# Routing in four parts instead of three, experts an earlier unit, and four more units masked by GpSimd

## The chip, the cores and the metric

One core of a Trainium2 chip runs the whole layer. The metric is the device time of one execution in microseconds. Three runs of the kernel before gave 662.93, 663.86 and 665.39 us.

## The reference, cut to what matters

4096 tokens (16 sequences of 256) of 128 channels are normalised, and the result goes into two branches whose outputs are added to the input: causal attention with 16 heads of 8 channels and a second layernorm, and a mixture of 8 experts of which each token takes its best two.

```python
xn  = layernorm(x)                                     # x: 16 x 256 x 128
Q, K, V = relu(xn @ Wq + bq), relu(xn @ Wk + bk), relu(xn @ Wv + bv)
att = softmax(causal(Q_h @ K_h.T / sqrt(8))) @ V_h     # 16 heads, rows whose sum of xn is 0 masked
att = layernorm(att + xn) * gamma + beta
h   = rms_weight * xn * rsqrt(mean(xn*xn) + 1e-6)
top_w, top_i = top_k(softmax(h @ gate_w.T), 2)         # weights scaled to sum 1
moe = sum over the two experts e: top_w * (silu(h @ w1[e].T) * (h @ w3[e].T)) @ w2[e].T
out = x + att + xn + moe
```

## The kernel before, in words

Tokens are cut into 32 tiles of 128, four tiles are a block (two sequences), so there are 8 blocks. Attention runs over 16 units: unit `u` is block `u // 2` with one half of the heads. A unit has these steps in a hand-written order: `weights(u, 0..2)` (scores transposed, with the maximum already folded in, and their exponentials `e` by ScalarE, L858), `scores(u+1, 0..2)` (scores of the next unit, only to find the row maxima: `tops`, L774 and L782 on VectorE), `values(u, 0..1)` (exponentials times V, `O`, copied to `oT` by ScalarE, L897), `finish(u, 0..1)` (division, second layernorm's statistics) and `queries(u+1)` (the maxima added to the queries, `Qs`, L800). The order of TensorE's instructions is the order of the program; a scheduler orders the other engines, with some orders fixed by hand (`behind`, `issue_after`).

In between, `fill()` is called seven times a unit and doles out other work by small budgets:

- `early_work` runs `prepared()`: for each chunk of tiles in `CHUNKS` the layernorm `normed` (ends with a square root by three Newton steps in `newton_sqrt`), and when the logits of a part in `ROUTES` are there, `route` (best two experts of each token, positions in the experts' lists by two small matmuls `pos_ps` and `taken_ps`, L548 to L555) and `planned` (which tiles of 256 list rows a wave of experts has). Each `yield` names its cost, and a fill may spend `EARLY_US` of it; `PAUSE` ends the fill's share. `logit_step` turns a normed block (`lT`, L662) and multiplies it with the gate (L657) one fill later.
- `masks` runs `exact`, an exact remainder of the layernorm that block n's attention needs; before the attention of a new block starts, what it needs is forced (in the even units).
- `spaced_rows` scatters tokens' rows into the experts' lists in DRAM by GpSimd (`lists<-rows`, L608, two per tile), `ROWS_BESIDE` of them per fill, held behind the last exponential.
- `experts` takes one step per `1 / EXPERT_STEPS` fills. An expert tile `i` (36 tiles of 256 rows are always worked) takes three steps: `deliver` of tile i-2 (`R_ps`, `fres`, two scatters with addition into `places`, L1137), the first half of `up` (`AG`, L1100), `down` of tile i-1 (`Y`, L1117), turning of tile i+1 (`hT_ps`, L1089), the second half of `up`. `fetch(i)` loads the rows of tile i from the lists (`frows`, SyncE's queue, L1068) and the three weights; if the plan of tile i is not there yet, it forces `early_work`, and it forces all scatters of the parts that the tile's wave needs. `WAVES` follows from `ROUTES`: tile i belongs to the first wave whose routed tokens must fill it.
- `rest` does the second layernorm's last part (L1195 to L1202).

The experts' generator is made in unit `EXPERTS_FROM` and starts `EXPERTS_BEHIND` steps in debt. After the last unit the experts that are left run alone, with two steps of `rest` after each of theirs; then `places` is read back (`z`, L1345), added (L1349) and written out. In units before `POOL_MASKS` the causal mask of the exponentials is added by TensorE before the exponential (L847, 12 small bf16 matmuls with the identity a unit); from there on GpSimd zeroes the masked exponentials afterwards (L861, 6 selects a unit), and `values` waits for them.

Of the kernel before, what the change touches and what calls it, by code (L numbers as in the profile page):

```python
# [26 lines left out]
def tile_attention_plus_moe(  # L27
# [47 lines left out]
    NR = H // (HG * NG)  # L75

    ONE, OFF = 16, 18
    CHUNKS = [(0, 4), (4, 16), (16, 32)]
    ROUTES = [(0, 16), (16, 24), (24, 32)]
    RT = 16  # L80

    FIRST_US, EARLY_US, MASK_US, EXPERT_STEPS = 4.5, 1.4, 1.0, 1.08
    EXPERTS_FROM, EXPERTS_BEHIND = 2, 3
    ROWS_BESIDE = [3, 2, 1]
    POOL_MASKS = 7
    QSCALE = float(DH) ** -0.5
    SL = 256
    NTILES = (2 * NTOK + E * (SL - 1)) // SL  # L90
# [193 lines left out]
    def newton_sqrt(yv, w, tag):  # L284

        s = small.tile([P, w], F32, tag=f"{tag}s", name=f"{tag}_s")
        V.tensor_scalar(s[:].bitcast(U32), yv.bitcast(U32), 1, None, ALU.logical_shift_right)
        V.tensor_scalar(s[:].bitcast(U32), s[:].bitcast(U32), float(0x1FBD1DF5), None, ALU.add)
        rr = small.tile([P, w], F32, tag=f"{tag}r", name=f"{tag}_r")
        for _ in range(3):  # L290
            yield 0.8
            V.reciprocal(rr, s)
            V.tensor_tensor(rr, rr, yv, ALU.mult)
            V.tensor_tensor(s, s, rr, ALU.add)
            V.tensor_scalar(s, s, 0.5, None, ALU.mult)
        V.reciprocal(rr, s)
        return s, rr

# [7 lines left out]
    def misc(name):  # L306
        return psM.tile([P, BW], F32, tag="misc", name=name)
# [45 lines left out]
    PAUSE = None  # L353
# [136 lines left out]
    def route(t0, t1):  # L490

        n, nt = f"c{t0}", t1 - t0
        rs = rstd[:, t0:t1]
        lg = small.tile([P, nt, E], F32, tag="rlg", name=f"rlg_{n}")
        V.tensor_tensor(
            lg, lraw[:, t0:t1, :], rs.unsqueeze(2).to_broadcast([P, nt, E]), ALU.mult
        )

        sel = norm.tile([P, 2, nt, E], F32, tag="rsel", name=f"rsel_{n}")
        mx = small.tile([P, 2, nt], F32, tag="rmx", name=f"rmx_{n}")  # L500
        nth = small.tile([P, nt, E], F32, tag="rnth", name=f"rnth_{n}")
        for r in range(2):
            V.tensor_reduce(mx[:, r, :], lg, AX.X, ALU.max)
            V.tensor_tensor(
                sel[:, r], lg, mx[:, r, :].unsqueeze(2).to_broadcast([P, nt, E]), ALU.is_equal
            )
            yield 0.6
            V.tensor_tensor_scan(
                nth.rearrange("p t e -> p (t e)"),
                of_token[:, 0:nt, :].rearrange("p t e -> p (t e)"),  # L510
                sel[:, r].rearrange("p t e -> p (t e)"),
                0.0,
                ALU.mult,
                ALU.add,
            )
            V.scalar_tensor_tensor(sel[:, r], nth, 1.0, sel[:, r], ALU.is_equal, ALU.mult)
            if r == 0:
                V.scalar_tensor_tensor(lg, sel[:, r], MASKED, lg, ALU.mult, ALU.add)
            yield 0.9

        wts = small.tile([P, 2, nt], F32, tag="rwts", name=f"rwts_{n}")
        ex = small.tile([P, nt], F32, tag="rex", name=f"rex_{n}")
        V.tensor_tensor(ex, mx[:, 1, :], mx[:, 0, :], ALU.subtract)
        S.activation(ex, ex, AF.Exp)
        yield 0.2

        mine_bf = small.tile([P, E, nt], BF16, tag="rmine", name=f"rmine_{n}")
        V.tensor_tensor(
            mine_bf,
            sel[:, 0].rearrange("p t e -> p e t"),  # L530
            sel[:, 1].rearrange("p t e -> p e t"),
            ALU.add,
        )
        upto = small.tile([P, E, nt], BF16, tag="rupto", name=f"rupto_{n}")
        V.tensor_tensor_scan(
            upto.rearrange("p e t -> p (e t)"),
            going[nt].rearrange("p e t -> p (e t)"),
            mine_bf.rearrange("p e t -> p (e t)"),
            0.0,
            ALU.mult,  # L540
            ALU.add,
        )
        V.tensor_scalar(wts[:, 0, :], ex, 2.0, 2.0, ALU.mult, ALU.add)
        V.reciprocal(wts[:, 0, :], wts[:, 0, :])
        V.tensor_tensor(wts[:, 1, :], wts[:, 0, :], ex, ALU.mult)
        yield PAUSE
        pp = misc(f"pos_ps_{n}")[:, : E * nt]
        T.matmul(  # L548
            pp, lhsT=behind_bf, rhs=mine_bf.rearrange("p e t -> p (e t)"), start=True, stop=False
        )  # L550
        T.matmul(
            pp, lhsT=ones_bf, rhs=upto.rearrange("p e t -> p (e t)"), start=False, stop=True
        )
        tp = misc(f"taken_ps_{n}")[:, :E]
        T.matmul(tp, lhsT=ones_bf, rhs=upto[:, :, nt - 1], start=True, stop=True)  # L555
        begin = small.tile([P, E], F32, tag="rbegin", name=f"rbegin_{n}")
        V.tensor_tensor(begin, taken, list_start, ALU.add)
        V.tensor_tensor(taken, taken, tp, ALU.add)
        pos = small.tile([P, nt, E], F32, tag="rpos", name=f"rpos_{n}")
        V.tensor_tensor(  # L560
            pos,
            pp.rearrange("p (e t) -> p t e", e=E),
            begin.unsqueeze(1).to_broadcast([P, nt, E]),
            ALU.add,
        )
        yield 0.6
        pick = norm.tile([P, 2, nt, E], F32, tag="rpick", name=f"rpick_{n}")
        at = small.tile([P, 2, nt], F32, tag="rat", name=f"rat_{n}")
        at_u = small.tile([P, 2, nt], U32, tag="ratu", name=f"ratu_{n}")
        V.tensor_tensor(pick, sel, pos.unsqueeze(1).to_broadcast([P, 2, nt, E]), ALU.mult)  # L570
        V.tensor_reduce(at, pick, AX.X, ALU.add)
        V.tensor_copy(at_u, at)
        yield 1.1
        part = ROUTES.index((t0, t1))
        rows_left.append((part, scattered(part, t0, at_u, wts)))
# [658 lines left out]
    def fill(k_next=0):  # L1234

        logit_step(normed_upto[1])
        normed_upto[1] = normed_upto[0]
        due["early"] += EARLY_US if tiles_at else FIRST_US
        while due["early"] > 0:
            cost = beside(early_work)  # L1240
            if not cost:
                due["early"] = 0.0
            else:
                due["early"] -= cost
        due["masks"] = min(due["masks"] + MASK_US, 2 * MASK_US)
        while due["masks"] > 0 and exact_upto[0] < rooted_upto[0]:
            due["masks"] -= beside(masks)
        spaced_rows()
        for _ in range(k_next):
            next(side["next"], None)  # L1250
        due["experts"] += EXPERT_STEPS
        while due["experts"] >= 1:
            due["experts"] -= 1
            next(side["experts"], None)
        beside(side["rest"])
# [18 lines left out]
    for u in range(len(units)):  # L1274
        n, r = units[u]
        more = u + 1 < len(units)

        due_next = [0, 0, 0, 0, 1, 1, 1] if r == 0 else [1, 1, 1, 1, 0, 0, 0]
        if u == EXPERTS_FROM:
            side["experts"] = experts(ffn_pool, 0, USUAL)  # L1280
            due["experts"] = -EXPERT_STEPS * EXPERTS_BEHIND
        weights(u, 0)
        for _ in first:
            pass
        fill(due_next[0])
        if more:
            scores(u + 1, 0)
        fill(due_next[1])
        if u == EXPERTS_FROM:
            next(side["experts"])  # L1290
        weights(u, 1)
        fill(due_next[2])
        if more:
            scores(u + 1, 1)
        fill(due_next[3])
        if more:
            scores(u + 1, 2)
        o0 = values(u, 0)
        if r == 0 and n + 1 < NB:
            while exact_upto[0] < n + 2:  # L1300
                logit_step()
                beside(masks if rooted_upto[0] > n + 1 else early_work)
            side["next"] = projected(n + 1)
        fill(due_next[4])
        weights(u, 2)
        finish(u, 0, o0)
        if more:
            queries(u + 1)
        fill(due_next[5])
        o1 = values(u, 1)  # L1310
        exps.pop((u, 0))
        fill(due_next[6])
        finish(u, 1, o1)
        if r == 0 and n in (5, 7):
            for _ in side["rest"]:
                pass
            side["rest"] = rest(0, 4) if n == 5 else rest(4, 6)
    side["rest"] = chain(side["rest"], rest(6, 8))
    for _ in side["experts"]:
        for _ in range(2):  # L1320
            next(side["rest"], None)
    for _ in side["rest"]:
        pass

# [78 lines left out]
```

## Time and profile before

| | us |
|---|---|
| median of three runs | 663.86 |
| profiled execution, whole | 665.17 |
| its span in the profile | 663.30 |
| TensorE busy (matmuls) | 545.0 |
| VectorE busy | 435.9 |
| ScalarE busy | 337.8 |
| GpSimd busy | 246.6 |

The profile starts 1.87 us short of the device time. The first exponential of each unit starts at 50.05, 101.47, 141.50, 178.19, 218.09, 263.24, 298.89 and 331.74 us (units 0 to 7); unit 15 starts at 600.04 us. "Before 50 us" is the first block's layernorm, "after 623.9 us" the last experts alone and the way out.

### The profile page before, as it was taken

The numbers are of one execution on the slowest core, as the hardware profiler recorded it, in microseconds if no ns is written. First come the engines' busy times: TensorE is split into PE (matmuls) and PEld (weight loads), VectorE is DVE, ScalarE is ACT, GpSimd is POOL, SyncE is SP. The second block draws the span as 40 slices with busy tenths as digits, with TensorE's granted clock in tenths as the row PEclk, the third lists the DMA queues.
The fourth block names the chain that finished last, engine by engine and source line by source line (L and its number), as shares of the span: only waits on it lengthen the run. The fifth ranks groups of instructions, "written<-read, shape, count | busy, mean of one in ns | idle before, by whom it ended". The sixth has DMA issues, their size and how long they took to land. (4 is left out here: it accounts for less than half of the span.)

```text
span 663.3 us, 9975 instructions
## 1 busy us (share of the span) xinstructions
PE 545.0 (82%) x3293; PEld 323.9 (49%) x3293; DVE 435.9 (66%) x1171; ACT 337.8 (51%) x677; POOL 246.6 (37%) x287
## 2 busy tenths in 40 slices
PE   0377867687998968999999999899989998999940
PEld 0134523234665545556555655565655565566620
DVE  6757686576378675667666766786587656575943
ACT  1524597145735615555556456545668554445620
POOL 4240027460012554445352434243524244435450
PEclk9997669777999979999999999999999999999975
DMA  7200001015122342354323323332333223234128
GB/s 200 94 1 0 1 13 45 28 41 162 51 50 55 82 95 66 86 127 129 67 65 69 102 59 62 70 100 59 63 70 96 50 71 75 65 93 116 17 21 257
DMA packets 45892, 49.33 MB, mean 74 GB/s; under 512 B 5840, under 2 KB 38224, under 8 KB 45840
## 3 DMA queue, kind: packets, MB, share of 16 engines
q1 hardware_dynamic: 30112, 37.40, 18.8%
q0 software_dynamic: 12416, 8.99, 9.8%
q10 hardware_dynamic: 3312, 2.30, 1.2%
q8 instruction: 27, 0.44, 0.3%
q14 instruction: 25, 0.20, 0.1%
HBM read 34.16 MB, written 14.50 MB: 73 GB/s over the span
## 5 line engine op out<-in xcount | busy, mean ns | idle before, releaser
L1137 POOL DMA_INDIRECT places<-fres,frows x72 | 115.1, 1599 | 172.1 <-DVE fres L1133 143.1
L1100 PE MATMUL AG<-hT,w 128*112 128x256 f32 x576 | 140.0, 386 | 6.0 <-PE R_ps L1131 3.8
L1100 PEld LDWEIGHTS AG<-hT,w 128*112 128x112 f32 x576 | 98.5, 178 | 38.8 <-issue 9.9
L858 ACT ACTIVATE e<-W 128x1024 f32<-128x1024 f32 x96 | 93.3, 1020 | 46.4 <-PE W L847 27.7
L782 DVE TENSOR_REDUCE tops<-S 128x4 f32<-128x1024 f32 x64 | 75.3, 1217 | 37.2 <-PE S L760 26.7
L1109 DVE SCALAR_TENSOR_TENSOR th<-th,AG 112x512 f32<-112x512 f32 x72 | 49.4, 686 | 71.5 <-ACT th L1108 68.0
L608 POOL DMA_INDIRECT lists<-rows,ratu_c x64 | 64.1, 1001 | 57.8 <-ACT e L858 28.3
L1117 PE MATMUL Y<-hid,w 112*128 112x256 f32 x288 | 72.9, 397 | 13.8 <-ACT oT L897 5.0
L861 POOL TENSOR_SCALAR_AFFINE_SELECT e<-e 128x512 f32<-128x512 f32 (+1 forms) x54 | 49.6, 977 | 86.0 <-ACT e L858 85.7
L1108 ACT ACTIVATE th<-AG 112x512 f32<-112x512 f32 x72 | 42.8, 594 | 61.9 <-PE AG L1100 57.8
L747 PE MATMUL S<-KTm,QT 32*128 32x256 f32 (+1 forms) x512 | 67.9, 543 | 6.7 <-DVE tops L782 4.9
L832 PE MATMUL W<-Qm,KT 32*128 32x512 f32 (+1 forms) x512 | 65.6, 550 | 9.1 <-DVE tops L774 4.9
L1117 PEld LDWEIGHTS Y<-hid,w 112*128 112x128 f32 x288 | 53.7, 195 | 29.5 <-ACT oT L897 6.6
L1111 DVE TENSOR_TENSOR hid<-th,AG 112x512 f32<-112x512 f32 x72 | 48.9, 679 | 1.6
L897 ACT COPY oT<-O 128x512 f32<-128x512 f32 x32 | 18.7, 584 | 60.3 <-PE O L887 41.9
L774 DVE TENSOR_REDUCE tops<-S 128x8 f32<-128x1024 f32 x32 | 37.7, 1218 | 12.8 <-remote 8.1
L747 PEld LDWEIGHTS S<-KTm,QT 32*128 32x128 f32 x512 | 29.7, 193 | 33.1 <-issue 12.8
L876 PE MATMUL O<-e,vstat 128*32 128x512 f32 x256 | 36.3, 639 | 5.1 <-ACT yT L1125 2.6
L760 PE MATMUL S<-cmask,ident_bf 128*128 128x256 bf16 (+1 forms) x192 | 38.7, 327 | 0.0
L832 PEld LDWEIGHTS W<-Qm,KT 32*128 32x128 f32 x512 | 25.9, 195 | 25.2 <-issue 6.7
L1125 ACT COPY yT<-Y 128x256 f32<-128x256 f32 x36 | 13.3, 370 | 45.8 <-PE Y L1117 43.4
L760 PEld LDWEIGHTS <-ident_bf 128*128 128x128 bf16 x192 | 15.3, 100 | 36.7 <-issue 32.4
(236 smaller groups left out, 768.6 us busy)
## 6 DMA issues: line engine op xcount, KB each, us to landing
w<-in_w1T_dram SPq DMA_DIRECT2D x36, 224.0 KB
w<-in_w3T_dram SPq DMA_DIRECT2D x36, 224.0 KB
w<-in_w2T_dram SPq DMA_DIRECT2D x36, 224.0 KB
frows<-lists SPq DMA_DIRECT2D x36, 130.0 KB
places<-nought SPq DMA_DIRECT2D x8, 256.0 KB
lists<-filling SPq DMA_DIRECT2D x9, 130.0 KB
places<-fres,frows POOLq DMA_INDIRECT x72
lists<-rows,ratu_c POOLq DMA_INDIRECT x64
```

What stands on the lines that cost most here:

```text
L608: ins = G.indirect_dma_start(out=lists, out_offset=bass.IndirectOffsetOnAxis(ap=at_u[:, r, b - t0 + t : b - t0 + t + 1], axis=0), in_=rows ...
L747: T.matmul(out, lhsT=QT[rows, q0 : q0 + P], rhs=KTm[rows, :, b * SEQ : b * SEQ + nk], start=(part < 2 or b == 0), stop=False, skip_group_c ...
L760: T.matmul(out, lhsT=ident_bf, rhs=cmask[:, 0, :].unsqueeze(1).to_broadcast([P, 4 if part == 2 else 2, P]), start=False, stop=True, skip_g ...
L782: ins = V.tensor_reduce(of_heads[:, :, part, 1, :], pairs[g // 2].rearrange("p g (j k) -> p g j k", j=HG), AX.X, ALU.max, negate=True,).ins
L832: T.matmul(out, lhsT=KT[rows, k0 : k0 + P], rhs=Qm[rows, :, k0 : (b + 1) * SEQ], start=(part > 0 or b == 0), stop=on_pool and (part > 0 or ...
L858: ins = S.activation(two, pairs[g // 2], AF.Exp).ins
L861: behind["POOL"] = G.affine_select(on, on, [[0, 2 * nd], [1, P]], ALU.is_ge, no_weight, base=0, channel_multiplier=-1).ins
L1100: T.matmul(to[:, ts(c, SL)], lhsT=wt[:, 0, ts(2 * k + c, CI)], rhs=hT, start=True, stop=True,)
L1109: V.scalar_tensor_tensor(th, th, 1.0, ap, ALU.add, ALU.mult)
L1111: V.tensor_tensor(h, th, gp, ALU.mult)
L1117: T.matmul(yp, lhsT=w2[:, 0, c, :], rhs=hid[c // 2][:, ts(c % 2, SL)], start=(c == 0), stop=(c == NCI - 1),)
L1137: ins = G.indirect_dma_start(out=places, out_offset=bass.IndirectOffsetOnAxis(ap=rows[:, a, C : C + 1].bitcast(U32), axis=0), in_=res[:, a ...
```

## The change

Four things are edited, and constants with them.

1. `CHUNKS` goes from three chunks of 4, 12 and 16 tiles to four of 4, 8, 8 and 12; `ROUTES` from parts of 16, 8 and 8 tiles to parts of 12, 8, 8 and 4. The waves of expert tiles become [5, 13, 21, 39] instead of [9, 17, 39]. `EARLY_US` goes from 1.4 to 2.2, and a part after the first pauses once more before its position matmuls.
2. The experts' generator is made after fill 5 of unit 1 and at once takes its first step (the fetch of tiles 0 and 1), two steps in debt; before, it was made in unit 2, fetched after its second fill, three steps in debt.
3. `POOL_MASKS` goes from 7 to 3: units 3 to 6 are masked by GpSimd too.
4. A Newton step of the square root has two fused VectorE instructions and a reciprocal instead of three instructions and a reciprocal. After the last unit one step of `rest` follows each expert step instead of two.

```diff
-    CHUNKS = [(0, 4), (4, 16), (16, 32)]
-    ROUTES = [(0, 16), (16, 24), (24, 32)]
-    RT = 16
+    CHUNKS = [(0, 4), (4, 12), (12, 20), (20, 32)]
+    ROUTES = [(0, 12), (12, 20), (20, 28), (28, 32)]
+    RT = 12
...
-    FIRST_US, EARLY_US, MASK_US, EXPERT_STEPS = 4.5, 1.4, 1.0, 1.08
-    EXPERTS_FROM, EXPERTS_BEHIND = 2, 3
-    ROWS_BESIDE = [3, 2, 1]
-    POOL_MASKS = 7
+    FIRST_US, EARLY_US, MASK_US, EXPERT_STEPS = 4.5, 2.2, 1.0, 1.08
+    EXPERTS_FROM, EXPERTS_BEHIND = 1, 2
+    ROWS_BESIDE = [3, 2, 2, 1]
+    POOL_MASKS = 3
...
         for _ in range(3):
-            yield 0.8
+
+            yield 0.6
             V.reciprocal(rr, s)
-            V.tensor_tensor(rr, rr, yv, ALU.mult)
-            V.tensor_tensor(s, s, rr, ALU.add)
-            V.tensor_scalar(s, s, 0.5, None, ALU.mult)
+            V.scalar_tensor_tensor(rr, yv, 0.5, rr, ALU.mult, ALU.mult)
+            V.scalar_tensor_tensor(s, s, 0.5, rr, ALU.mult, ALU.add)
...
         yield PAUSE
+        if t0 > 0:
+            yield PAUSE
         pp = misc(f"pos_ps_{n}")[:, : E * nt]
...
-        if u == EXPERTS_FROM:
-            side["experts"] = experts(ffn_pool, 0, USUAL)
-            due["experts"] = -EXPERT_STEPS * EXPERTS_BEHIND
         weights(u, 0)
...
-        if u == EXPERTS_FROM:
-            next(side["experts"])
         weights(u, 1)
...
         fill(due_next[5])
+        if u == EXPERTS_FROM:
+            side["experts"] = experts(ffn_pool, 0, USUAL)
+            next(side["experts"])
+            due["experts"] = -EXPERT_STEPS * EXPERTS_BEHIND
         o1 = values(u, 1)
...
     for _ in side["experts"]:
-        for _ in range(2):
-            next(side["rest"], None)
+        next(side["rest"], None)
```

Built, the two programs differ in their order as follows. In unit 0 TensorE has three turned blocks of logits instead of four ahead of `xnT_1`. The first expert matmul (`AG` of tile 0) stands in unit 2 after the first `scores` part instead of after the second; at the start of unit 7 the new order has one half of `up` and one `down` more behind it, at the start of unit 15 two halves of `up`. The logits of blocks 4 to 7 move from units 2 and 3 to units 1, 2 and 4. On ScalarE the eight L1195 of the last two blocks stand behind the last expert's tanh instead of ahead of it.

## The prediction

> **What bounds the kernel now.** I read the page's 40 slices first, to see where TensorE has no work.
>
> ```profile
> PE   0377867687998968999999999899989998999940
> DVE  6757686576378675667666766786587656575943
> POOL 4240027460012554445352434243524244435450
> PEclk9997669777999979999999999999999999999975
> ```
>
> From slice 16 (265 us) to slice 37 TensorE is busy nine tenths at full clock: there only fewer matmuls shorten the run. From 33 to 265 us no engine is full, and the clock granted to TensorE is often 0.6 or 0.7. The windows of the units say how far each is from full (columns: us, busy of PE, PEld, DVE, ACT, POOL, then clock, DMA share, GB/s).
>
> ```profile
> 50.00:101.50 51.50, 39.60 (x201) 20.76 (x198) 38.24 (x148) 34.37 (x93) 4.99 (x9) 0.70 0.02 6
> 101.50:141.50 40.00, 27.90 (x144) 12.67 (x143) 24.58 (x66) 15.80 (x33) 24.82 (x30) 0.80 0.12 39
> 141.50:178.20 36.70, 31.45 (x186) 16.79 (x185) 20.58 (x53) 22.56 (x50) 4.83 (x5) 0.89 0.34 104
> 178.20:218.10 39.90, 36.30 (x247) 23.12 (x246) 29.05 (x109) 19.23 (x37) 9.02 (x9) 1.00 0.22 48
> 218.10:263.20 45.10, 36.51 (x220) 22.36 (x219) 30.04 (x93) 20.39 (x41) 23.70 (x26) 0.92 0.34 85
> 263.20:298.90 35.70, 33.63 (x220) 20.76 (x219) 22.49 (x63) 20.71 (x43) 15.29 (x17) 1.00 0.44 103
> 298.90:331.70 32.80, 31.69 (x206) 19.48 (x204) 23.22 (x51) 17.31 (x31) 15.43 (x13) 1.00 0.39 97
> ```
>
> Units 0 to 4 are the expensive ones. Who waited for whom, with the longest single wait last:
>
> ```profile
> DVE tops L774 <- remote: 8.1, 1, 8.1
> ACT oT L897 <- remote: 15.8, 2, 8.0
> PE hT_ps L1089 <- DMA frows<-lists: 3.6, 1, 3.6
> PE Y L1117 <- DVE hid L1111: 4.7, 1, 4.7
> ```
>
> The first two are two holes, at 118 to 126 us (unit 1) and 235 to 243 us (unit 4): VectorE and ScalarE wait for matmuls that by their recorded starts were long done. No row names a cause; both lie in runs of list scatters on GpSimd. The third is the first expert waiting for its rows in unit 2, the last a delay in the tail.
>
> **The change, unit by unit.** I take each unit's length in the profile and work out what it loses and gains.
>
> Ahead of unit 0: three Newton steps lose one instruction of 0.20 us spacing each, 0.6; GpSimd sets up two more small memsets that VectorE's L950 stands behind, +0.2. Unit 0 begins at 49.7 instead of 50.05.
>
> Unit 0 (51.4 us). In the timeline each turned block of logits costs TensorE 3.55 us:
>
> ```profile
> 77.64 1.09 PE L662 MATMUL lT_ps<-ident,xn 128*128 128x128 f32 x4
> 79.47 1.88 PE L657 MATMUL logit_ps<-gws,lT 128*128 128x8 f32 x8 [0.73 <-ACT lT L664]
> 81.19 1.09 PE L672 MATMUL xnT_ps<-ident,xn 128*128 128x128 f32 x4
> 90.97 0.27 PE L548 MATMUL pos_ps_c<-rmine_c,behind_bf 128*128 128x128 bf16 x1 [5.15 <-DVE Qs L800]
> ```
>
> One of four is gone: -3.55. VectorE has one square and scan less (0.65 + 1.15), and its Newton steps now stand ahead of a maximum; of that 1.4 reach TensorE, whose next `scores` then wait for the maximum. Between the last logits and `Qs`, on which TensorE waits 5.15, VectorE has 8.9 us of work; two additions of 0.69 move ahead and the part is 12 tiles wide: 6.9 left, -2.0. From `Qs` on nothing changes. Sum -7.0: 44.4.
>
> Unit 1 (40.0). Two waits for `remote`, 2.4 and 8.1, make its hole of 10.5; without it 29.5. TensorE gets lT_3, logits 3 and lT_4, about 3 us at the half clock. VectorE's work goes from 28.3 to 29.3 us (mean spacing of each form times the number of instructions): 32.5 without the hole, 43.0 with it. The trace shows the hole and no reason; the new order has the same run of eight scatters behind the same exponential. I count half, 37.7, and keep 0 and 10.5 as bounds.
>
> Unit 2 (36.7). The fetch moves up with its forced scatters and eight SyncE transfers, which wait for the last of them; part 0 has 24 scatters instead of 32 at 1.27 us spacing, 10.2 less of GpSimd's queue, and the last of them are due about 9 us after the last exponential of unit 1, ahead of the first expert matmul: the waits of 3.55 and 0.73 go. If the rows are late, the 4.3 come back. lT_4 and lT_5 leave (-1.0), one half of `up`, one `down`, an `hT` and the second part's position matmuls come (1.8 + 1.8 + 0.3 + 0.5). 35.8.
>
> Masks in units 3 to 6. Off TensorE go 4 matmuls of 512 columns and 8 of 256 a unit, spaced 0.88 and 0.45 per four at full clock: 1.78 a unit, 7.1 in all (the groups' busy time, part of it at half clock, would make 10.5). On GpSimd come 6 selects a unit.
>
> ```profile
> L861 POOL TENSOR_SCALAR_AFFINE_SELECT e<-e 128x512 f32<-128x512 f32 x36 | 26.9, 831 | 54.4 <-ACT e L858 54.3
> L861 POOL TENSOR_SCALAR_AFFINE_SELECT e<-e 128x1024 f32<-128x1024 f32 x18 | 22.6, 1271 | 31.6 <-ACT e L858 31.4
> ```
>
> That is 4 x 0.831 + 2 x 1.271 = 5.9 us a unit, beside the matmuls as in units 7 to 15. `values` waits for them; behind a select that waits for its exponential stand list and result scatters, and behind a blocked result scatter stand selects. In unit 5 GpSimd's queue holds 14 list scatters (17.8), three pairs of results at 1.9 each (11.4) and the selects: 35.1 us.
>
> The shortest and longest L861 of 54 are 0.627 and 1.668 us. [...]
>
> Unit 3 (39.9): one half of `up` more (+1.8), logits 5 to 7, two turnings and a wait for one gone (-4.5), masks -1.8: 35.4 for TensorE. But chunk and second part now fall here, and VectorE's instructions from `Qs` to `Qs` rise from 27.6 to 34.5 us; in order, between matmuls, it will not run without holes, so I add 4: 38.5 (bounds 35.4 and 41).
> Unit 4 (45.1): one half of `up` and one `R_ps` less (-2.1), logits 5 to 7 with turnings +3.8, masks -1.8: 45.0 with the hole of 8.0, 37.0 without; half: 41.
> Unit 5 (35.7): masks -1.8, position matmuls and a turning +0.8, so 34.6; VectorE from 25.7 to 34.0 because parts three and four end here; plus 4: 38 (bounds 34.6 and 41).
> Unit 6 (32.9): masks only, 31.1.
> Units 7 to 14 (268.3): the same instructions in nearly the same order. Unchanged. The second pause in `route` puts position matmuls of later parts one fill later; by the order no expert's fetch stands within half a unit of them, so it costs nothing here, and a late plan would hold SyncE's queue and with it the next weights.
>
> Tail. Unit 15 begins two halves of `up` further on (-3.9), so `R_ps` of tile 34 ends 29.4 after its first exponential instead of 33.3. Result scatters follow each other by 5.75 us in the tail (623.90, 629.67, 635.42); the last came at 642.86, 7.44 later, because eight L1195 of 0.40 us and VectorE's `rest` stood ahead of the last tanh, hence the 4.7 us wait of `Y`. They move behind it, where VectorE idles 9.65 us anyway for `z`. Last scatter at 29.4 + 0.8 + 5.75 = 35.9 after unit 15's begin instead of 42.8: -6.9. What follows it, 20.4, stays.
>
> Sum: 49.7 + 44.4 + 37.7 + 35.8 + 38.5 + 41 + 38 + 31.1 = 316.2 at unit 7 (331.7 before); + 268.3 + 35.9 + 20.4 = 640.8 span, + 1.9 = 642.7 device time of a profiled execution against 665.17. The median is 1.3 below that execution: 641.
>
> **Rivals.** First: both holes recur. Then units 1 and 4 get 5.3 and 4.0 more: 650. For it: same scatters, same code. Against: scatters and matmuls meet at other moments. Second: no hole: 632. Third: VectorE or GpSimd takes most of the gain in units 1 to 6, as 34 us of ordered work in a 35 us unit suggests; with the holes kept and 4 us lost in each of units 3 and 5, 658. Fourth, slower: the selects sit behind result scatters, which wait for the pair before them to land. If in units 3 to 6 each of 12 parts costs `values` one pair (3.8 us), that is 45.6, and 641 becomes 687; it outweighs the rest from 1.9 us a part on. For it: GpSimd's 35 us in unit 5. Against: L861 in units 7 to 15, where the same queue holds results too and TensorE never waits for POOL in the table of waits. Fifth: nothing changes, since the experts' first matmul moves only from behind the second `scores` part of unit 2 to behind the first, and its rows could still be late: that alone would leave the shorter unit 0 and tail, so a whole "same" needs the other losses too, 662.
>
> **How the numbers follow.** Forecast 0.46, both holes 0.20, no hole 0.12, third rival 0.10, slower 0.08, same 0.04. 0.5% is 3.3 us, about what a measurement of this kernel can tell from no change. All but the last two are faster: 0.88. The low end is no hole with units 3 and 5 at TensorE's own length (632 - 3.1 - 3.4 = 625), the high end the third rival: 625 to 658.
>
> **What would show it.** In the profile after: unit 1's first exponential near 94 us; no wait of `hT_ps` for `frows`; first exponentials of units 3 to 7 near 168, 206, 247, 285 and 316; L847 x12 shapes for three units only, L861 x78; `R_ps` of the last tile with no wait of `Y` for `hid` above 2 us. It is wrong if TensorE waits for POOL `e` in units 3 to 6, if units 3 or 5 exceed 41, or if the units after 7 lengthen.

## The result, and the profile after

The changed kernel took **672.95 us** (median of 4 runs, 668.75 to 678.36) beside 664.56 us of the kernel before on the same chip: ratio **1.0138, 95% interval 1.0092 to 1.0184, so slower**, where 641 us was forecast. The profiled execution is the longest, 678.36 us with a span of 676.7. In code after L547 its lines are two higher than before (L800 is L802). The page's slices after:

```profile
PE   0477875788888989879899979997988999999940
DVE  6657765667398786847566746667476736574763
POOL 4340057202583345665343424342323442345450
PEclk9986687799898989889999989998999999999985
```

From slice 20 (338 us) on, where TensorE was busy nine tenths at full clock, there are now 7s and 8s, and the clock has dips at slices 23 and 27. The units' windows show where the time went (columns as in the prediction):

```profile
49.10:96.70 47.60, 39.33 (x189) 19.66 (x186) 35.48 (x140) 28.76 (x74) 5.88 (x11) 0.71 0.02 6
96.70:139.10 42.40, 29.57 (x157) 15.04 (x159) 23.88 (x88) 17.43 (x35) 19.70 (x23) 0.76 0.24 74
139.10:179.80 40.70, 33.30 (x196) 18.68 (x195) 24.19 (x84) 25.16 (x59) 8.72 (x14) 0.92 0.21 61
179.80:219.60 39.80, 34.53 (x209) 21.20 (x210) 33.38 (x106) 20.66 (x42) 24.84 (x20) 0.96 0.33 76
219.60:258.70 39.10, 35.66 (x234) 22.87 (x234) 29.21 (x92) 21.36 (x44) 15.61 (x18) 0.96 0.29 67
258.70:301.40 42.70, 36.14 (x212) 21.99 (x213) 30.67 (x109) 19.63 (x39) 29.44 (x29) 0.93 0.47 105
301.40:336.40 35.00, 30.93 (x194) 18.91 (x195) 20.23 (x41) 18.63 (x36) 17.36 (x17) 0.99 0.33 78
336.40:371.00 34.60, 32.54 (x209) 19.94 (x211) 23.07 (x58) 19.51 (x39) 14.06 (x12) 1.00 0.33 73
371.00:408.50 37.50, 32.38 (x193) 19.65 (x195) 23.44 (x50) 16.53 (x28) 11.92 (x10) 0.95 0.27 61
```

Unit 7 begins at 336.4 us, 4.6 later than before instead of 15.5 earlier. The last row is unit 8: 37.5 us instead of 32.3, with TensorE's 193 matmuls busy 32.38 us and the clock at 0.95. Units 7 to 14, the same instructions as before, take 280.9 us instead of 268.3: **12.6 us** more. The span grew by 13.4: the other parts nearly cancel, with units 0 to 6 together 5.6 us longer, the start 0.95 and the tail 3.8 us shorter. Within units 7 to 14 TensorE waited for `Qs` like this, before (first three rows) and after (last two; us in total, times, longest):

```profile
PE Y L1117 <- DVE Qs L800: 3.3, 3, 1.3
PE q_ps L679 <- DVE Qs L800: 2.7, 3, 1.2
PE R_ps L1131 <- DVE Qs L800: 1.0, 1, 1.0
```
```profile
PE q_ps L681 <- DVE Qs L802: 8.1, 3, 3.7
PE R_ps L1133 <- DVE Qs L802: 3.8, 4, 1.0
```

That is 7.0 us before and 11.9 after. With its other waits, TensorE's idle time in these units rose from 14.8 to 22.7 us, and its busy time from 253.5 to 258.1 us, although the instructions are the same.

`queries` turns the maxima on TensorE, VectorE adds them to the queries (`Qs`), and TensorE's next product needs that PSUM tile back. The timeline of VectorE in unit 8 shows what stands in its queue there (start, length, operation; some rows left out):

```profile
389.20 0.68 DVE L471 TENSOR_TENSOR r<-r,p 128x512 f32<-128x512 f32 x1
389.87 0.42 DVE L1135 TENSOR_TENSOR fres<-R_ps,frows 128x256 f32<-128x256 f32 x1
390.93 1.14 DVE L475 SCALAR_TENSOR_TENSOR y<-r,ninv_c,xn 128x128 f32<-128x128 f32 x4
392.23 0.69 DVE L1111 SCALAR_TENSOR_TENSOR th<-th,AG 112x512 f32<-112x512 f32 x1 [0.16 <-ACT th L1110]
392.97 0.68 DVE L1113 TENSOR_TENSOR hid<-th,AG 112x512 f32<-112x512 f32 x1
393.56 2.78 DVE L325 TENSOR_TENSOR lacc_s<-lacc_s,y 128x64 f32<-128x64 f32 x6
396.63 0.63 DVE L802 TENSOR_TENSOR Qs<-QT,top_ps 128x512 f32<-128x512 f32 x1
```

TensorE had turned the maxima by 393.65 us; it waits until 397.31 for `Qs`, behind exact means and masks (`r`, `y`, `lacc_s`) and an expert's result and hidden rows (`fres`, `th`, `hid`). And it pays twice. TensorE's windows around that wait (us, busy, granted clock, DMA):

```profile
391.00:393.60 2.60, 2.60 (x19) 1.00 0.28 25
393.60:397.30 3.70, 0.05 (x1) 1.00 0.20 18
397.30:399.00 1.70, 1.69 (x3) 0.61 0.34 78
399.00:401.00 2.00, 2.00 (x6) 0.50 0.00 0
401.00:403.00 2.00, 1.67 (x14) 0.98 0.00 0
```

After 3.7 idle us the clock is at half for some 3.4 us by these rows, which costs about 1.7 us more, an estimate: half of the 3.4. The same happens once more in unit 10, after a wait of 3.5 us (clock 0.54 from 469.2 to 471 us and 0.56 from 471 to 473), so by the same estimate some 3.4 us of the longer busy time are the clock. Shorter waits were followed by half clock too, as the last section shows.

What stands ahead of `Qs` changed because the experts' steps start earlier. Their count advances by 1.08 a fill, 7.56 a unit, and three steps make a tile, so 15.1 steps, about five tiles, fall into two units and the pattern nearly keeps its phase. The change moved it by two fills, 2.16 steps. Unit 8 in TensorE's order, the names of unit and tile left out (`AG`, `Y,hT` and `R,AG` are the experts' three steps), before and after:

```
before  W_0 R,AG  S_0 Y,hT  W_1 AG  S_1 R,AG  S_2 O_0 xnT Y,hT  W_2 o top q AG    O_1 k R,AG o
after   W_0 AG    S_0 R,AG  W_1 Y,hT  S_1 AG  S_2 O_0 xnT R,AG  W_2 o top q Y,hT  O_1 k AG   o
```

Ahead of `top` stood `Y,hT`, which is ScalarE's work; now stands `R,AG`, which is VectorE's, and in even units the forced exact means stand there too, as they did before the change, when TensorE waited 1.2 us for `Qs` in unit 8.

### The profile page after: what moved, and what is told of

Its sections match the earlier page's. It is cut to its first block, busy times and chain, and to the rows that moved or that the text cites. A ratio compares the mean times of both kernels' runs of the same rounds, so it can differ in the third digit from the quotient of the medians.

```text
span 676.7 us, 9978 instructions
## 1 busy us (share of the span) xinstructions
PE 547.0 (81%) x3235; PEld 324.8 (48%) x3248; DVE 439.9 (65%) x1237; ACT 338.0 (50%) x678; POOL 270.0 (40%) x325
## 4 chain that ended last, share of the span: by engine, by line
PE 54%; DVE 22%; ACT 10%; DMA 6%; issue 4%; another core or an unknown queue 1%; POOL 1%; SPq 0%; ACTq 0%; DVEq 0%; POOLq 0%
PE AG L1102 14%; PE Y L1119 8%; PE S L749 6%; PE W L834 5%; PE O L878 4%; DMA places<-fres,frows 4%; PE S L762 4%; DVE tops L784 3%; PE q_ps L681 2%; DVE tops L776 2%; ACT e L860 2%; PE k_ps L694 2%; DVE th L1111 2%; DVE hid L1113 2%; PE O L889 2%
## 5 line engine op out<-in xcount | busy, mean ns | idle before, releaser
L1139 POOL DMA_INDIRECT places<-fres,frows x72 | 119.4, 1659 | 102.1 <-DVE fres L1135 60.0
L863 POOL TENSOR_SCALAR_AFFINE_SELECT e<-e 128x512 f32<-128x512 f32 (+1 forms) x78 | 67.6, 939 | 143.3 <-ACT e L860 143.2
L749 PE MATMUL S<-KTm,QT 32*128 32x256 f32 (+1 forms) x512 | 70.3, 548 | 14.9 <-issue 6.8
L1119 PEld LDWEIGHTS Y<-hid,w 112*128 112x128 f32 x288 | 55.8, 200 | 26.9 <-issue 7.8
L749 PEld LDWEIGHTS S<-KTm,QT 32*128 32x128 f32 x512 | 30.2, 193 | 41.7 <-issue 18.2
L776 DVE TENSOR_REDUCE tops<-S 128x8 f32<-128x1024 f32 x32 | 37.6, 1218 | 7.8 <-PE S L762 7.1
L878 PE MATMUL O<-e,vstat 128*32 128x512 f32 x256 | 38.3, 672 | 1.7 <-ACT yT L1127 1.7
L608 POOL COPY rows<-rwts_c 128x4 f32<-128x4 f32 x16 | 4.1, 254 | 77.9 <-DVE rwts_c L544 49.6
L681 PE MATMUL q_ps<-xnT,wq_sb 128*128 128x512 f32 x32 | 22.4, 791 | 13.8 <-DVE Qs L802 13.0
```

The costliest lines, as they stand in the source:

```text
L749: T.matmul(out, lhsT=QT[rows, q0 : q0 + P], rhs=KTm[rows, :, b * SEQ : b * SEQ + nk], start=(part < 2 or b == 0), stop=False, skip_group_c ...
L863: behind["POOL"] = G.affine_select(on, on, [[0, 2 * nd], [1, P]], ALU.is_ge, no_weight, base=0, channel_multiplier=-1).ins
L878: T.matmul(op[rows, :], lhsT=v[:, 2 * b, r * NG + g, :], rhs=e0[:, g, :], start=True, stop=False, skip_group_check=True, tile_position=(0, ...
L1119: T.matmul(yp, lhsT=w2[:, 0, c, :], rhs=hid[c // 2][:, ts(c % 2, SL)], start=(c == 0), stop=(c == NCI - 1),)
L1139: ins = G.indirect_dma_start(out=places, out_offset=bass.IndirectOffsetOnAxis(ap=rows[:, a, C : C + 1].bitcast(U32), axis=0), in_=res[:, a ...
```

## The experiments

The kernels ran on several chips, each beside the kernel before on the same one, so the verdicts are ratios. The kernel before itself took 664.6 us in the first comparison and on the chip of E9 to E12, and 647 us on three other chips; E5 shows why. The table has the lengths of the units in the profiles, in us, from first exponential to first exponential; the tail runs from unit 15's to the end. The runs on chips with the two holes of the prediction (the first comparison, E9 to E12) are left out.

```
                                     start  u0   u1   u2   u3   u4   u5   u6  u2-6  u7-14 tail  span  ratio (95%)
before (E5)                           50.6 50.9 29.7 37.4 39.9 37.6 35.7 32.8 183.4 268.3 63.8 646.7
changed (E6)                          49.0 47.6 28.7 40.7 41.7 38.8 36.3 36.6 194.1 280.6 59.0 659.0 1.0225 (1.0198-1.0252)
E1  changed, steps in old order       49.1 45.3 31.7 38.6 40.9 38.5 41.1 33.1 192.2 268.7 64.1 651.2 1.0036 (1.0006-1.0066)
E2  before, steps in new order        50.7 50.7 27.9 50.9 40.4 37.0 35.3 35.1 198.7 277.8 58.6 664.5 1.0334 (1.0303-1.0364)
E3  changed, TensorE masks            50.2 44.7 33.0 41.2 40.7 38.0 36.8 36.8 193.5 280.7 59.7 661.9 1.0207 (1.0170-1.0244)
E4  before + Newton at 0.6 + rest     50.5 50.4 29.0 37.0 43.8 43.4 34.7 32.8 191.7 268.3 63.2 653.2 1.0128 (1.0099-1.0156)
E7  E1 with TensorE masks             50.1 45.4 31.8 38.6 41.2 39.5 40.5 33.9 193.7 268.7 63.6 653.2 1.0125 (1.0093-1.0156)
E8  before + GpSimd masks             49.4 52.3 29.7 35.6 42.0 39.1 34.9 32.1 183.7 268.3 64.2 647.6 1.0048 (1.0027-1.0070)
E13 E1 with old routing               49.2 51.4 29.7 37.2 42.3 44.2 35.9 32.1 191.7 268.3 63.9 654.2 1.0140 (1.0120-1.0160)
E14 before + Newton, rest, masks u5-  49.2 51.4 29.7 37.1 39.9 37.1 35.0 32.1 181.2 268.3 62.1 641.9 0.9967 (0.9955-0.9978)
E15 before + Newton at 0.8 + rest     49.1 50.9 29.7 37.2 39.9 37.6 35.6 32.8 183.1 268.3 63.6 644.6 0.9999 (0.9986-1.0012)
E16 E13 without second pause          50.2 50.9 27.8 39.2 42.1 39.2 34.9 32.1 187.5 268.3 64.2 648.9 1.0053 (1.0037-1.0069)
E17 E1 without second pause           49.1 47.6 28.7 35.1 41.5 45.3 40.4 33.1 195.4 268.7 64.0 653.6 1.0144 (1.0124-1.0163)
E18 E1, GpSimd masks from unit 5      50.1 44.9 28.7 38.6 41.1 39.0 40.2 33.1 192.0 268.7 62.3 646.7 1.0049 (1.0031-1.0068)
```

**The phase of the experts' steps.** E1 changes one number of the changed kernel, E2 one of the kernel before. With it TensorE's order from unit 6 on is the other kernel's, apart from the masks of unit 6.

```diff
-    EXPERTS_FROM, EXPERTS_BEHIND = 1, 2      # E1, in the changed kernel
+    EXPERTS_FROM, EXPERTS_BEHIND = 1, 4
-    EXPERTS_FROM, EXPERTS_BEHIND = 2, 3      # E2, in the kernel before
+    EXPERTS_FROM, EXPERTS_BEHIND = 2, 1
```

> The whole change, but the experts' count of owed steps starts two steps lower (EXPERTS_BEHIND 4), so that from unit 6 on TensorE's instructions stand in exactly the order of the kernel before. Theory A (the order of the experts' steps against the attention steps costs the 12.6 us of units 7 to 14): units 7 to 14 take 268 to 271 us instead of 280.9, and as two halves of `up` (3.9 us) fall back behind the last unit, the time is 672.95 - 12.6 + 3.9 = about 664 us. Theory B (something else of the change, such as GpSimd's queue, the planner's order on VectorE or the clock, slows those units): they stay near 281 us and the time is 673 to 677 us.

> The kernel before with one edit, EXPERTS_BEHIND 1 instead of 3: experts start two steps earlier, and from unit 6 on TensorE's instructions stand in exactly the order of the changed kernel; routing, masks, Newton steps and tail stay. Theory A: units 7 to 14 take about 281 us instead of 268.3, less 3.9 us of `up` that no longer stands behind the last unit: 664.6 + 12.6 - 3.9 = about 673 us. Theory B: units 7 to 14 stay at 268 us, and the time is 661 to 664.6 us.

Units 7 to 14 took 268.7 us in E1 and 277.8 in E2: theory A both ways, and the tail went the other way as expected. E1 takes back the whole lengthening; E2 makes 9.5 of its 12.3 us, since unit 10 stays at 32.5 us there (36.4 in E6). E2's ratio is worse than the changed kernel's because its first expert waits 11.6 us for `frows` in unit 2, which the other parts of the change avoid. Same windows of waits, E1 and then E2, from 330 to 600 us:

```profile
PE q_ps L681 <- DVE Qs L802: 2.9, 3, 1.2
```
```profile
PE q_ps L679 <- DVE Qs L800: 5.7, 3, 3.6
PE R_ps L1131 <- DVE Qs L800: 3.8, 4, 1.0
```

**Order on TensorE, or VectorE's queue?** E9 and E12 keep the changed kernel's TensorE order and only do the exact means earlier.

```diff
-    FIRST_US, EARLY_US, MASK_US, EXPERT_STEPS = 4.5, 2.2, 1.0, 1.08
+    FIRST_US, EARLY_US, MASK_US, EXPERT_STEPS = 4.5, 2.2, 1.4, 1.08   # E9; E12: 2.4
```

> The changed kernel with one number, MASK_US 1.4 instead of 1.0: the exact means and masks of later blocks (r, y, lacc on VectorE) are done in more of the steps before and no longer all at once ahead of `queries`. TensorE's instructions stand in exactly the changed kernel's order. Between the last maximum and `Qs` VectorE then has 5 instead of 18 instructions in unit 8 and 8 instead of 25 in unit 10. Theory A (the lengthening of units 7 to 14 is TensorE's wait for `Qs` behind VectorE's queue, and the half clock after it): units 8 and 10 fall from 37.4 and 36.4 us to 33, units 7 to 14 from 280.6 to about 273, ratio 1.010 of before instead of 1.0225. Theory B (TensorE's own new order is the slower one): units 7 to 14 stay at 280 us, ratio 1.02.

> The changed kernel with MASK_US 2.4 instead of 1.0, TensorE's order again that of the changed kernel. Between the last maximum and `Qs` VectorE has 5, 5 and 8 instructions in units 6, 8 and 10 instead of 16, 18 and 25, but 29 and 44 in units 3 and 5 (44 and 45 in the changed kernel). Theory A: units 6, 8 and 10 fall to about 33 us each, 36.6 + 37.4 + 36.4 before, so 11 us, some of it paid back in units 1 to 5, which take over the masks' work: ratio 1.007. Theory B (TensorE's own order): units 7 to 14 stay at 280 us, ratio 1.02 or above.

Both ran on a chip with holes, which disturb units 0 to 5. In E12 units 6, 8 and 10 took 32.7, 32.3 and 32.3 us and units 7 to 14 together 270.6; its waits in the same window:

```profile
PE R_ps L1133 <- DVE Qs L802: 3.8, 4, 1.0
PE q_ps L681 <- DVE Qs L802: 3.8, 4, 1.0
```

So 10 of the 12.3 to 12.6 us are the queue ahead of `Qs`, which theory A says; the other 2.4 stay with the new order (units 11 to 14 take 136.7 us in both, 134.3 before). In E9 units 8 and 10 fell to 32.3 each, but unit 7 rose to 41.8, as another pile came to stand ahead of its `Qs` (`R_ps` waits 3.7 us for it): 277.8 in all, a partial miss. In time, ratios were 1.0266 (1.0171 to 1.0362) for E9, above both theories, and 1.0165 (1.0089 to 1.0240) for E12: the means done earlier pile up in units 2 to 5, where E12 takes 39.0, 39.4, 46.2 and 44.8 us.

**The two holes.** E5 is the kernel before, E6 the changed one, again.

> The kernel before itself, for a profile of it beside the next three. On the chip of the first four experiments it took 647 us instead of 664.6. Theory A (the two holes in units 1 and 4, 10.5 and 8 us, in which ScalarE and VectorE wait for matmuls that by their records are done, belong to some executions or chips and not to the program): where it takes about 647 us, both holes are gone, unit 1 lasts about 29.5 us and unit 4 about 37, the other units are as before within 1 us. Theory B (the whole run is faster, for instance by the clock): the holes are there and every unit is shorter.

> The changed kernel itself, beside the same runs of the kernel before as the next two. The first four experiments say what to expect relative to before: the whole change with the experts' steps in the old order stood at 1.0036; the new order costs 12 us in units 7 to 14 and gives back 3.9 us behind the last unit, so 1.016 (about 657 us where before takes 647). If its own three holes (6.8 us in unit 1, 5.7 us in unit 4) were what made it slow against before, it is at most 1.00.

The holes were not there: unit 1 lasts 29.7 us instead of 40.0 and unit 4 37.6 instead of 45.2, the others are as before, and no engine waits for `remote` as long as 1.5 us; no profile of these three chips but E3's (2.6 us) has such a wait. Each profile taken where the kernel before took 664 us has them, in other places too. In the changed kernel of the first comparison:

```profile
ACT oT L899 <- remote: 5.7, 1, 5.7
DVE tops L784 <- remote: 5.5, 2, 4.6
```

So, by six profiles with waits for `remote` over 4 us and fourteen without, they go with the chip and not with the program. What they are stays open. Without them the change is slower still, 1.0225.

**The masks.** E3, E7 and E8 move one number: E3 in the changed kernel, E7 in E1's, E8 in the kernel before.

```diff
-    POOL_MASKS = 3      # E3, E7
+    POOL_MASKS = 7
-    POOL_MASKS = 7      # E8
+    POOL_MASKS = 3
```

> The change without the moved masks (POOL_MASKS 7 again, units 3 to 6 masked by TensorE). Theory A of the prediction (each of units 3 to 6 gains 1.78 us by the move): units 3 to 6 take 156.5 + 7.1 = 163.6 us, and the time rises to 680 us. Theory B (VectorE and GpSimd bound those units, the matmuls taken away were hidden by their waits): units 3 to 6 stay within 2 us of 156.5, the time stays at 673 us. Theory C (the selects delay `values`): units 3 to 6 get shorter, the time is below 670 us.

> The change with the experts' steps in the old order (as in the first experiment, 1.0036 of before) and also with the masks of units 3 to 6 on TensorE again. Theory A (the moved masks gain 1.78 us a unit): units 3 to 6 take 153.6 + 7.1 = 160.7 us, the time is 1.014 of before. Theory B (GpSimd's selects, waiting behind list and result scatters, cost as much as the matmuls): units 3 to 6 within 2 us of 153.6, ratio 1.000 to 1.007. Theory C (they cost more): units 3 to 6 below 151 us, ratio below 1.000.

> The kernel before with one edit, POOL_MASKS 3 instead of 7: masks of units 3 to 6 by GpSimd. Theory A (1.78 us a unit off TensorE): ratio 0.989 of before. Theory B (GpSimd's selects delay `values` by as much): ratio 0.998 to 1.002. Theory C (more): above 1.002, with unit 5 or 6 lengthened and a wait of TensorE for VectorE's or GpSimd's work behind a select.

Beside its counterpart, units 2 to 6 with masks on GpSimd are longer by 0.3 us (E8), longer by 0.6 (the changed kernel beside E3) and shorter by 1.5 (E1 beside E7). Not one of the three shows the gain of 7.1. In times the move costs half a per cent (E8), nothing (E3 beside E6) and gains 0.9% (E7 beside E1). The last is unsure: E7's units agree with its theory B and its ratio is near theory A's, and E1's ten runs lie between 644.7 and 655.1 us. E8's ratio is theory C's, but the units that grew are 3 and 4, not 5 or 6. Units 3 and 4 of the kernel before, and then of E8:

```profile
168.60:208.50 39.90, 36.30 (x247) 23.12 (x246) 29.04 (x109) 19.24 (x36) 9.01 (x9) 1.00 0.22 48
208.50:246.10 37.60, 34.21 (x219) 21.12 (x218) 29.73 (x93) 20.59 (x41) 23.78 (x24) 1.00 0.41 101
```
```profile
167.00:209.00 42.00, 36.39 (x236) 23.20 (x235) 30.22 (x108) 19.45 (x36) 13.73 (x15) 0.96 0.20 45
209.00:248.20 39.20, 34.40 (x208) 21.04 (x208) 30.27 (x94) 20.62 (x42) 28.00 (x31) 0.96 0.39 96
```

Eleven matmuls fewer in each, and TensorE is as long busy as before: it comes to the point where it waits for VectorE sooner, waits longer (2.0 and 2.3 us for `Qs` at `pos_ps_c`, 1.3 and 1.5 before), and the clock falls to 0.96. In units 5 and 6, at full clock, the same move gains 0.8 and 0.7 us.

**Newton steps and `rest`.** E4 does both in the kernel before; E11, and E15 on another chip, count a Newton step at 0.8 us again.

```diff
-            yield 0.6      # E4
+            yield 0.8      # E11, E15
             V.reciprocal(rr, s)
             V.scalar_tensor_tensor(rr, yv, 0.5, rr, ALU.mult, ALU.mult)
```

> The kernel before with only the fused Newton steps and the single step of `rest` behind each step of the experts at the end; routing, masks and the experts' start stay. By the prediction's terms: start -0.6, unit 0 -1.4, tail -3.0 (the last result no longer waits for eight L1195 on ScalarE, `up` is where it was): 659.6 us. Rival: the order that the planner makes elsewhere moves as well, and units in between lengthen by as much: 664 to 666 us.

> As the fourth experiment (the kernel before with fused Newton steps and one step of `rest`, 1.0128), but each Newton step is still counted at 0.8 us instead of 0.6, so that the early work falls into the same fills as before; VectorE's instructions ahead of `Qs` in units 2 to 6 are those of the kernel before. Theory A (the fourth experiment lost its 8 us in units 3 and 4 because the new count moved early work into the fill ahead of `queries`): units 3 and 4 return from 43.8 and 43.4 us to about 40 and 37.6, and the ratio is 0.995 to 0.999. Theory B (the fused instructions or the single step of `rest` cost it): the ratio stays near 1.012.

> The eleventh experiment's kernel again, on the chip of the two above: the ratio there was 0.9955 with an interval that reached 0.9997. Theory A (0.6 to 2 us in the start and unit 0, 1 us in the tail): 0.994 to 0.998. Theory B (that ratio was the chip's scatter): 0.999 to 1.002.

E4 lost 8 us, in units 3 and 4, which neither its forecast nor its rival had; with the old count they are back, and the ratio is 0.9955 (0.9914 to 0.9997) in E11 and 0.9999 in E15. So the cheaper code is worth about nothing here, and the 0.2 in its `yield` cost 8 us, since it decides into which fill the early work falls: in E4 TensorE's `pos_ps_c` and `taken_ps_c` stand elsewhere in two places than in the kernel before, in E15 nowhere. E15 corrects E11.

**The early work in units 2 to 6.** Five attempts, all on the changed kernel with the steps in old order: E10 issues no early and no mask work in the one fill ahead of `queries`; E13 takes back chunks, parts and pace; E16 and E17 take out the second pause, with old and new routing; E18 moves masks from unit 5 only.

```diff
-        fill(due_next[4])                    # E10, and in fill: while early and due["early"] > 0
+        fill(due_next[4], u < 1)
-        if t0 > 0:                           # E16, E17
-            yield PAUSE
-    ROUTES = [(0, 12), (12, 20), (20, 28), (28, 32)]      # E13, E16, and CHUNKS, RT, ROWS_BESIDE,
+    ROUTES = [(0, 16), (16, 24), (24, 32)]                # EARLY_US and Newton's 0.8 with it
-    POOL_MASKS = 3                                        # E18
+    POOL_MASKS = 5
```

> The change with the experts' steps in the old order (1.0036 of before), and in the one fill ahead of `queries` no early and no mask work is issued from unit 1 on; what is owed is done in the next fill. VectorE's instructions between the last maximum and `Qs` fall from 24 to 7 in unit 2 and from 39 to 19 in unit 5, and stay at 35 to 37 in unit 3. Theory A (TensorE waits for `Qs` behind early work): unit 5 falls from 41.1 to about 36 us (its wait of 3.7 us and the half clock behind it), unit 3 keeps its wait of 4.9 us, ratio about 0.996. Theory B (the sum of VectorE's work bounds units 2 to 5, whatever its order): the sum of units 2 to 6 stays within 2 us of 192.2 and the ratio near 1.003.

> The change without its routing: chunks, three parts, pace (EARLY_US 1.4, Newton steps counted at 0.8 us) and the order of the experts' steps as before; left of the change are the moved masks, the fused Newton steps, the earlier fetch and the single step of `rest`. Theory A (in the change four parts put more VectorE work ahead of `Qs` in units 2 to 6, and that, not the masks, takes what unit 0 gains): units 2 to 6 fall from the 192.2 us of the first experiment to about 184 on a chip without the two holes, unit 0 rises from 45.3 to 50 us, ratio 0.995 to 1.000. Theory B (the moved masks and the earlier fetch lengthen units 2 to 6): units 2 to 6 stay at 190 us or more, ratio above 1.003.

> As the thirteenth experiment (old routing, old order of steps, 1.014), with the change's second pause in `route` taken out as well; VectorE's instructions ahead of `Qs` are then those of the kernel before in every unit. Left of the change: masks by GpSimd from unit 3, earlier fetch, fused Newton steps, single step of `rest`. Theory A (the pause puts the later parts' plan one fill on, and the work that comes late then stands ahead of `Qs` and of SyncE's fetches in unit 4): unit 4 falls from 44.2 to about 39 us, as with the masks alone, and the ratio to 1.003 to 1.006. Theory B (masks or the earlier fetch): unit 4 stays at 43 us or more, ratio 1.012.

> As the first experiment (the change with the old order of steps, 1.0036), without the second pause in `route`. Theory A (the pause costs in units 2 to 6): VectorE has 15 instead of 39 instructions ahead of `Qs` in unit 5 but 39 instead of 11 in unit 4, so unit 5 falls from 41.1 to about 36 us and unit 4 rises from 38.5 by less; ratio 0.997 to 1.001. Theory B (the clump only moves from unit 5 to unit 4): the sum of units 2 to 6 stays within 2 us of 192.2, ratio 1.003.

> As the first experiment (1.0036), with masks by GpSimd from unit 5 instead of unit 3. Theory A (moved masks cost in units 3 and 4 and gain in 5 and 6, as in the kernel before): units 3 and 4 fall by 1 to 3 us together, ratio 0.999 to 1.002. Theory B (here, as the seventh experiment says with 1.0125, TensorE's masks cost in every unit that has them): ratio 1.005 to 1.010.

E10, on a chip with holes, brought unit 5 from 41.1 to 38.8 us and kept 5.2 us of wait in unit 3; ratio 1.0073 (1.0039 to 1.0106), inconclusive, as a hole lies in units 1 and 3. E13 made units 2 to 6 no shorter (191.7), so the routing in four parts is not alone to blame, and it gave unit 0 its 6 us back: with old routing the change is worse, 1.0140. In E13's unit 4 TensorE waits like this (neither row is over 1.2 us there in the kernel before):

```profile
PE AG L1102 <- issue: 3.6, 2, 2.4
PE q_ps L681 <- DVE Qs L802: 3.5, 1, 3.5
```

E16 shows the pause to be the reason there: without it unit 4 falls from 44.2 to 39.2 us, what the masks alone leave (39.1 in E8), and 1.0140 becomes 1.0053. E17 shows the opposite sign with the new routing: without the pause unit 4 grows from 38.5 to 45.3 us while unit 5 falls only from 41.1 to 40.4 and unit 2 from 38.6 to 35.1; 195.4 us in all and 1.0144, worse than both of its theories. E18 left units 3 to 6 as they were, between both theories at 1.0049. What each part costs in units 2 to 6 is therefore not a sum: as far as the waits show, each shifts what VectorE has ahead of some `Qs`. That part is explained in kind and not split.

**A version that beats both.** E14 puts the parts that did not lose into the kernel before: fused Newton steps at the old count, one step of `rest`, masks by GpSimd from unit 5.

```diff
-    POOL_MASKS = 7      # in E15's kernel
+    POOL_MASKS = 5
```

> The kernel before with what the experiments leave as gains: fused Newton steps at the old count, one step of `rest` per step of the experts at the end, and masks by GpSimd from unit 5 on (POOL_MASKS 5), since with masks moved from unit 3 on units 3 and 4 lost 2.1 and 1.5 us and units 5 and 6 won 0.8 and 0.7. Theory A: the masks' 1.5 us add to the 0.9955 of the eleventh experiment: ratio 0.993. Theory B (GpSimd's queue of list scatters in unit 5 eats it): 0.9955 as the next run, or above.

645.0 us, ratio 0.9967 (0.9955 to 0.9978): faster than the kernel before by 2 us, a third of a per cent and less than theory A's 0.993, and than the changed one by 16 on such a chip. As E15 is at 0.9999, what it gains comes with the masks of units 5 and 6 (0.6 and 0.7 us in the profiles).

## Why the prediction was wrong, point by point

The forecast span was 640.8 us and the measured one 676.7, a miss of 36. Units 7 to 14 are 12.6 of it, units 0 to 6 together 21 and the tail 3. So two steps failed. The first is units 7 to 14, and it decides that the change is slower: with the old phase (E1) the ratio is 1.0036. The second is units 1 to 6, where savings on TensorE were taken as time: without holes the terms of units 2 to 6 add up to 180.4 us, E6 has 194.1 and E1, which corrects the first step alone, 192.2. So E1 gains nothing where 3.4% was forecast.

- **Units 7 to 14, "unchanged": the first step that failed.** 0 forecast, 12.6 us measured. "The same instructions in nearly the same order" was true of the instructions; the order differed in which expert's step stands ahead of `Qs`. E1 and E2 show the phase to be the cause, E12 that VectorE's queue carries 10 us of it (with the half clock behind the waits). The text named a lengthening after unit 7 as what would prove it wrong, but priced it at zero.
- **The holes.** I counted half of 10.5 and of 8 us as gains. They go with the chip (E5), so no share of them was a gain of the change. In the first comparison the changed kernel has its own: unit 1 takes 42.4 us there and 28.7 in E6.
- **Start and unit 0.** 0.35 and 7.0 forecast; 0.9 and 3.8 measured in the first comparison. The wait of `pos_ps_c` for `Qs` fell from 5.15 to 1.90 us, more than my 2.0; but the block of logits that left was busy time at a clock of 0.7, and TensorE's busy time in the unit stayed at 39 us at 0.71. In E1 and E18 the clock is 0.76 and 0.80 there and the unit 45.3 and 44.9 us, near the forecast 44.4.
- **Unit 2.** The wait for `frows` is gone, as forecast. In its place came 2.4 us of `q_ps` for `Qs` and 2.3 us of `hT_ps` for ScalarE's `QT`, and part of it at half clock: 40.7 us instead of 35.8.
- **Masks, 7.1 us: part of the second step.** The matmuls left and the time did not (E3, E7, E8). I took off TensorE's time at full clock in units where TensorE waits for VectorE.
- **Unit 6, "masks only", 31.1 us.** 35.0 measured, 36.6 in E6: 2.5 us of waiting for `Qs`, from the same phase as in units 8 and 10, since E1 has 33.1 and E12 32.7.
- **Units 3 and 5, "plus 4 for holes".** 39.8 and 42.8 us against 38.5 and 38 (41.7 and 36.3 in E6): the right reason, but the waits cost more than their length where the clock halves behind them (0.96 and 0.93 in these units). VectorE's work in units 2 to 6 grew from 124.9 to 138.1 us (sum of its busy column, E5 and E6).
- **Tail, 6.9 us.** 3.8 measured, 4.8 in E6. The 3.9 of `up` is there (E1, without it, has 64.1 us like before); the term that failed is the 3.0 on top of it. `Y` waits shorter, below the 2 us that I had named as a sign:

```profile
PE Y L1119 <- DVE hid L1113: 1.8, 2, 1.3
```

and `R_ps` of tile 34 ends 30.0 us after unit 15's begin, near the forecast 29.4. But I let its result scatter start 0.8 us behind it, at 30.2. It started at 32.3, 5.9 us behind the pair before it; the last pair followed by 5.9 more, and the way out took 21.2 us instead of 20.4. The profiles that have the new end without the earlier `up` (E1, E4, E7, E10, E11, E13 to E18) have tails of 62.0 to 64.3 us beside 63.3 and 63.8 of the kernel before, so it alone shows no clear gain.
- **The rivals.** The third (VectorE takes the gain in units 1 to 6) was right in kind, at 658 us too cheap. The fourth ended slower, by selects that make `values` late: no row of the changed kernel's waits has TensorE wait for GpSimd's `e`, so the right sign came from a mechanism that I had not listed.

## What to carry to other kernels

Where an order is made by counters and due times, moving the start of one stream shifts its phase against the others for the whole run: compare the order around each point where the bounding engine waits without slack, in the steady state too, before calling it unchanged. Work taken off the bounding engine brought nothing here where that engine then waits for another one's queue; look at what stands in that queue there. A cost number in a scheduler's `yield` is part of the program: change it separately from the code that it describes.

## What the runs showed of the hardware that I had not expected

Some waits here were dearer than their length. In four profiles (E4, E6, E13, E14) all nine waits of TensorE of 3.26 us or more between 130 and 610 us go with a clock of 0.50 that lasts on behind them. Worked out from the mean clock of the windows that cover 6.0 us behind each, with every moment taken as 0.5 or 1, it is at half there for 3.1 to 3.4 us in four cases and for 5.4 to 6.0 in five; of the nine from 1.7 to 2.5 us four were followed by it, and five were not. A wait of 1.47 us in E6, with one of 0.7 us close by, was followed by it too, one of 1.49 us in E14 was not.

The same program with the same instructions took 664.6 us in two places and 647 us on three other chips. In the profiles of the kernel before the difference is two stretches of 8 to 10 us in which ScalarE and VectorE wait for `remote` (8.1 us in the first, 8.0 in the second) although the matmuls they need are done by their records; no run here shows why.
